# A graph network's edge loop: one stage of each of ten groups per iteration, and a POOL that waits for its own gathers

## The chip, the cores and the metric

The kernel runs on one core of a Trainium2 chip. The engines named here are TensorE (PE, matrix products; PEld is its weight load), VectorE (DVE), ScalarE (ACT), GpSimd (POOL) and SyncE (SP, which here only issues transfers). Each engine works through its own queue of instructions in order; between engines there are semaphores. SBUF is the memory that engines work in, PSUM the small memory that PE writes to. The metric is the device time of one execution in microseconds, as the median of several runs.

## What is computed

One layer of message passing over 200000 edges and 12500 nodes of 64 features, all in float32. `ssp` is softplus minus log 2. Edges are sorted by `dst`; `src` is random.

```python
nodes = node_state[edges].reshape(num_edges, -1)            # rows of src and dst, 128 wide
gates = ssp(edge_state @ We1 + be1) @ We2 + be2
gates = gates * (1.0 - sigmoid(5.0 * (edges_distance - 3.5)))
h = ssp(nodes @ Wn1 + bn1) @ Wn2 + bn2
messages = h * gates
message_sum = zeros_like(node_state).at[edges[:, 1]].add(messages)
# then per node: out = layernorm(2 * x + (ssp(message_sum @ Ws1 + bs1) @ Ws2 + bs2)), eps 1e-5
```

## The kernel before

The edges are cut into 391 groups of 512, each of four slots of 128 edges (one edge per partition). For a group g the stages are these, with the lines of the kernel.

- **gather** (L204): POOL issues one indirect DMA per slot, which fetches 128 rows of x (256 bytes each) by `src_i` into the tile `xg`. A few slots (70 of all) are instead put together column by column from a transposed copy of x, by short copies on DVE and ACT (L259, `columns`): per iteration 8 columns on DVE and 16 on ACT. So most groups issue four gathers, the others three; 1493 in all.
- **load** (L216, L224): SP fetches the edges' features `eT` (every second group) and, for each half group, 42 rows of a table (x times the second half of Wn1, written to DRAM in the early iterations) into `wns`.
- **onehot** (L277, DVE): a 42 wide one-hot of the edge's dst relative to the half group's first dst, beside the gathered row in `xg`.
- **transposes** (L283, PE) of the four slots into the PSUM tile `tx`, and **xcopy** (L291, ACT) of it to SBUF.
- **layer 1** (PE): bias L296, edge part L301, node part L308, into the PSUM tile `z` of 768 columns. Ahead of the node part stands a matmul whose result is not used (L334, `busy_before_node`), or, in early iterations, the product for one chunk of the table.
- **exps** and **logs** (L322, L325, ACT): u = ln(1 + exp(z)); **softplus** (L330, DVE) takes u from SBUF and z from PSUM.
- **layer 2** (PE): bias L347, edge part L354, node part L359, into the PSUM tile `gh`; another unused matmul (L334 with `gh`) ahead of it.
- **hcut** and **message** (L368, L372, DVE): the gate times the cutoff times h, from `gh`.
- **scatter** (L376, PE): the one-hot times the messages, into columns of a later group's `z` that are free; **window** (L396, DVE) adds these 84 columns to `sums` in SBUF, reading them in PSUM.

When all edges of 512 nodes are in `sums`, a node block (L398 to L479) makes their output rows; its eleven parts are spread over iterations by the lists in `BLOCK_STEPS`.

The order is written out by hand. Iteration i of the loop (L688 to L746) holds transposes, layer 1, exps, logs and softplus of group i+1; layer 2, hcut and message of group i; scatter and window of group i−2; gather of group i+3 and load of group i+5. The last groups and the last node block are written out after the loop (L750 to L789). POOL's gathers have no wait of their own in the code except, for the first groups, on transposes; later the eight buffers of `xg` make them wait. PSUM tiles come in pairs: two of `z`, two of `tx`, two of `gh`.

Of the kernel before, what the change touches and what calls it, by code (L numbers as in the profile page):

```python
# [11 lines left out]
I32 = mybir.dt.int32  # L12
# [61 lines left out]
def slots_by_columns(NG):  # L74

    slots, taken = [], set()
    for queue in (1, 0):
        columns, n = COLUMNS[queue], 0
        for g in range(NG - 2):
            if (g - 3 - COLUMNS_FROM + 1) * columns >= (n + 1) * P and not {g - 1, g, g + 1} & taken:  # L80
# [12 lines left out]
def chunk_of(i, NCH):  # L93

    c = i + CHUNKS
    return c if i >= 0 and c < NCH else None


def nodes_ready(g, NCH):

    return min(NCH, CHUNKS * (1 + max(0, (g - LOADS) // CHUNKS))) * P


@with_exitstack
def gnn_resnorm_kernel(ctx: ExitStack, tc: tile.TileContext, a: dict, out: bass.AP, E: int):
# [10 lines left out]
    REST = LOADS + 2  # L116
# [9 lines left out]
    loads = inner.enter_context(tc.tile_pool(name="loads", bufs=LOADS + 2, side="right"))  # L126
# [44 lines left out]
    columns_at = const.tile([P, sum(columns_of)], I32, name="columns_at")  # L171
    wn1_twice = const.tile([P, 2 * D], F32, name="wn1_twice")
# [22 lines left out]
    def gather(g, part=range(K), needs=()):  # L195

        if part[0] == 0:
            xgs[g] = loads.tile([P, K, P], F32, name="xg", bufs=AHEAD + BEHIND)
        xg = xgs[g]
        for k in part:  # L200
# [3 lines left out]
            behind(note(("gather", g), nc.gpsimd.indirect_dma_start(  # L204
                out=xg[:, k, :D], out_offset=None, in_=x,
                in_offset=bass.IndirectOffsetOnAxis(ap=src_i[:, g, k : k + 1], axis=0))), *needs)
            needs = ()
# [3 lines left out]
    def load(g):  # L211
        old = ("scatter", g - LOADS - 4)
# [18 lines left out]
    column_at, columns_done, whole = [[], []], [0, 0], []  # L231
# [32 lines left out]
    def choose(pool):  # L264

        while whole:
            queue, g, k = slot = whole.pop(0)
# [6 lines left out]
    xTs, zs, us, ss, ghs, hs, msgs, scs = ({} for _ in range(8))  # L274
# [14 lines left out]
    def xcopy(g):  # L289
        xT = work.tile([DW, K, P], F32, name="xT", bufs=3)  # L290
        note(("xcopy", g), nc.scalar.copy(xT, xTs[g]))  # L291
        xTs[g] = xT.rearrange("f (t h) e -> f h t e", h=2)

    def layer1_bias(g, *needs):
        zs[g] = z_tile()
# [21 lines left out]
    every, edge, node = slice(0, 3 * HE), slice(0, HE), slice(HE, 3 * HE)  # L317

    def exps(g, part=every):
        if part.start == 0:  # L320
            us[g] = work.tile([P, 3 * HE], F32, name="u")
        nc.scalar.activation(us[g][:, part], z_of(g)[:, part], AF.Exp)  # L322

    def logs(g, part=every):
        nc.scalar.activation(us[g][:, part], us[g][:, part], AF.Ln, bias=one)  # L325

    def softplus(g, part=every):
        if part.start == 0:
            ss[g] = work.tile([P, 3, 2, P], F32, name="s", bufs=3)
        nc.vector.scalar_tensor_tensor(ss[g].rearrange("p i t e -> p (i t e)")[:, part], us[g][:, part], BIG,  # L330
                                       z_of(g)[:, part], OP.min, OP.max)
# [7 lines left out]
    opened = {}  # L339

    def busy_before_layer2(g):
        opened[g + 1] = gh_tile()
        busy(opened[g + 1][:, :P])

    def layer2_bias(g):
        gh = opened.pop(g) if g in opened else gh_tile()
# [19 lines left out]
    def hcut(g):  # L366
        hs[g] = work.tile([P, K, D], F32, name="h")
        nc.vector.tensor_mul(hs[g], ghs[g][:, 1], cut[:, g, :].to_broadcast([P, K, D]))  # L368

    def message(g):  # L370
        msgs[g] = work.tile([P, K, D], F32, name="msg", bufs=3)
# [26 lines left out]
    def node_block(first, n, pool):  # L398
# [7 lines left out]
        def tile3(name):  # L406
            return pool.tile([P, 2, 2, D], F32, name=name, bufs=3)[:p, :nq]
# [4 lines left out]
        def hidden(z):  # L412
            t["z"] = z[:, :HE]
            for q in range(nq):
                nc.tensor.matmul(t["z"], ws1[:, q].rearrange("f o d -> f (o d)"),  # L415
                                 sums[:, first + q * HE : first + (q + 1) * HE], start=q == 0, stop=q == nq - 1,
                                 skip_group_check=True)

        def fetch():
            t["y"] = tile3("y")  # L420
            nc.sync.dma_start(t["y"], x[rows, :].rearrange("(q p k) d -> p q k d", q=nq, k=2))
# [5 lines left out]

        def clamp():
            t["l"], t["zb"] = (pool.tile([P, HE], F32, name=name, bufs=2) for name in ("l_s", "zb"))
            nc.vector.tensor_scalar(t["l"], t["z"], packed["bs1"], BIG, OP.add, OP.min)  # L430
            nc.vector.tensor_scalar(t["zb"], t["z"], packed["bs1"], None, OP.add)
# [8 lines left out]
        def layer2(z):  # L440
            slots = t["l"].rearrange("f (p k) -> f k p", k=2)
            t["u"] = z[:p, :HE].rearrange("p (q k d) -> p q k d", q=2, k=2)
            nc.tensor.matmul(z[:p, :HE], ones3[:, :p], rs3.rearrange("q k d -> q (k d)"), start=True,
                             stop=False, skip_group_check=True)
            for k in range(2):
                nc.tensor.matmul(t["u"][:, :, k, :], slots[:, k, :p], ws2, start=False, stop=k == 1,  # L446
                                 skip_group_check=True)

        def add():
            nc.vector.scalar_tensor_tensor(t["y"], t["y"], 2.0, t["u"][:, :nq], OP.mult, OP.add)  # L450

        def square():
            t["y2"] = tile3("y2")
# [23 lines left out]
        return [Part(None, fetch), Part(hidden, clamp), Part(None, logs), Part(None, center), Part(None, ssp),  # L477
                Part(layer2, add), Part(None, square), Part(None, variance), Part(None, root), Part(None, scale),
                Part(None, store)]  # L479

    def node_part(part):
        if part.tensor:
            part.tensor(gh_tile())
        part.others()

    with tc.manual_schedule():
# [4 lines left out]
        xT = sums[: D + 1, : NCH * P].rearrange("d (c p) -> d c p", p=P)  # L491
# [3 lines left out]
        def load_x(first, last):  # L495
            nc.sync.dma_start(xT[:, first:last, :], a["xT"][:, first:last, :])

        dst_h = prep.tile([P, NR, HE], I32, name="dst_h")
# [5 lines left out]
        nc.sync.dma_start(src_i[:, :HEAD, :], cols[:, :HEAD, :])  # L504
        nc.scalar.dma_start(dst_h, a["dst_h"])
        load_x(0, CHUNKS)
        nc.scalar.dma_start(consts[:, :FIRST], a["consts"][:, :FIRST])
        nc.sync.dma_start(dst_i[:, :HEAD, :], targets[:, :HEAD, :])
# [5 lines left out]
        load_x(CHUNKS, 2 * CHUNKS)  # L514

        for g in range(AHEAD):
            gather(g)
# [24 lines left out]
        for c in range(CHUNKS):  # L542
            nc.tensor.matmul(ps[:, c, :], xT[:, c, :], wnb, start=True, stop=True)
# [4 lines left out]
        spread = prep.tile([P, NR, P], F32, name="spread")  # L548
        base_b = prep.tile([P, NR * P], F32, name="base_b")
# [66 lines left out]

        def highest():
# [10 lines left out]
        def far():  # L628
            ps = tx_tile()
# [13 lines left out]
        def chunk(c, z):  # L643
            if c % CHUNKS == 0:
                tbs[c // CHUNKS] = piece()
            nc.tensor.matmul(z, xT[:, c, :], wnb, start=True, stop=True, skip_group_check=True)
# [6 lines left out]
        cuts = [2 * CHUNKS, 4 * CHUNKS, 6 * CHUNKS, 9 * CHUNKS, 12 * CHUNKS, NCH]  # L653
        beside = {0: [lambda: nc.sync.dma_start(src_i[:, HEAD:, :], cols[:, HEAD:, :])],
                  1: [lambda: nc.sync.dma_start(columns_i, a["columns"]), load_wn1, lambda: load_xh(0)],
                  2: [lambda: load_xh(1), far], 3: [lambda: load_xh(2)], 4: [lambda: load_xh(3), places],
                  5: [lambda: load_x(cuts[0], cuts[1])],
                  6: [lambda: nc.sync.dma_start(dst_i[:, HEAD:, :], targets[:, HEAD:, :])],
                  7: [lambda: load_x(cuts[1], cuts[2])], 10: [lambda: load_x(cuts[2], cuts[3])],
                  13: [lambda: load_x(cuts[3], cuts[4])], 16: [lambda: load_x(cuts[4], cuts[5])]}  # L660
# [6 lines left out]
        with tc.tile_pool(name="finish", bufs=1) as finish:  # L667
            blocks = list(zip(node_blocks(N), block_steps(N, NG)))
            last = NG - 1
            parts, begun, complete, rest = {}, None, 0, []  # L670
# [5 lines left out]
            def behind_by(i):  # L676
                close = last - CLOSE
                return [g for g in ([i - 2] if i <= close else []) + ([i - 1] if i >= close else []) if g >= 0]

            for g in range(LOADS - 1):  # L680
                load(g)
            for g in range(2):
                onehot(g)
            lowest(1, NR)
            everywhere(1, NR)
            clear(0, CHUNKS)
            highest()
# [264 lines left out]
```

## Time and profile before

| | |
|---|---|
| median of 3 runs | 2370.89 us (2367.87 to 3131.28) |
| profiled execution, its own time | 2389.88 us |
| its span | 2388.1 us |
| mean granted clock of PE in it | 0.981 |
| PE busy | 1970.5 us, 83% of the span |
| ACT busy | 1511.2 us, 63% |
| POOL busy | 1417.0 us, 59% |
| DVE busy | 1293.9 us, 54% |
| DMA | 148.63 MB, 62 GB/s |

Times of single rows come from the profiled execution, and are to be set against its own time of 2389.88 us, not against the median. Busy time counts an engine's own operations: a wait, and the issue of a transfer by SP, are not in it. The time that POOL spends on an indirect DMA is the time to issue it; the transfer itself runs on the DMA engines, afterwards or beside. In rows of groups the columns are: line, engine, operation, output and inputs, shapes, number of instructions, busy time and mean in nanoseconds, and then the engine's idle time right ahead of these instructions, with what ended most of it.

### The profile page before, as it was taken

How to read it: one execution, taken by the hardware profiler on the slowest of the kernel's cores; microseconds unless marked ns; L12 is line 12 of the kernel's file. 1: busy time of each engine (PE TensorE's matmuls, PEld its weight loads, DVE VectorE, ACT ScalarE, POOL GpSimd, SP SyncE). 2: the span in 40 equal slices, each digit the busy share in tenths (PEclk: the TensorE clock that was granted, in tenths of full speed). 3: DMA queues.
4: the chain of work that ended last, by engine and by line, in shares of the span. 5: the costliest groups of instructions: out<-in, count | busy, mean ns of one | idle time of the engine just before them, and what ended most of it. 6: DMA issues, size and time to landing. Idle time of an engine off the chain costs nothing.

```text
span 2388.1 us, 48209 instructions
## 1 busy us (share of the span) xinstructions
PE 1970.5 (83%) x12897; PEld 1656.7 (69%) x12897; DVE 1293.9 (54%) x5966; ACT 1511.2 (63%) x7412; POOL 1417.0 (59%) x1497
## 2 busy tenths in 40 slices
PE   6788888888888888888888888888888888888877
PEld 4666677767776776677677667766777767777765
DVE  4355555555555555555555555555555555555544
ACT  3466666666666666666666666666666666666653
POOL 5665665666666666666666666665665666666650
PEclk9799999999999999999999999999999999999988
DMA  6332232322222222222222222222222222222220
GB/s 185 85 91 68 56 75 56 77 61 71 54 57 56 53 59 54 57 56 62 53 59 55 57 58 55 59 59 54 58 58 56 59 57 60 63 57 58 59 50 14
DMA packets 159679, 148.63 MB, mean 62 GB/s; under 512 B 40564, under 2 KB 108949, under 8 KB 159274
## 3 DMA queue, kind: packets, MB, share of 16 engines
q1 hardware_dynamic: 111194, 94.97, 14.4%
q0 software_dynamic: 47776, 49.02, 10.8%
q8 instruction: 109, 1.79, 0.3%
q14 instruction: 166, 1.36, 0.2%
q10 hardware_dynamic: 434, 1.50, 0.2%
HBM read 135.70 MB, written 9.62 MB: 61 GB/s over the span
## 4 chain that ended last, share of the span: by engine, by line
PE 80%; issue 13%; ACT 3%; DVE 2%; another core or an unknown queue 1%; DMA 0%; DVEq 0%; ACTq 0%
PE z L308 18%; PE gh L359 13%; PE z L376 10%; PE tx L283 10%; PE gh L354 7%; PE z L301 6%; PE gh L334 4%; PE gh L347 3%; PE z L296 3%; PE z L334 2%; ACT xT L291 2%; PE tx L415 1%; PE tx L446 1%; PE z L311 1%
## 5 line engine op out<-in xcount | busy, mean ns | idle before, releaser
L204 POOL DMA_INDIRECT xg<-in_x,src_i x1493 | 1416.8, 949 | 919.3 <-PE tx L283 488.8
L308 PE MATMUL z<-xT,wns 106*128 106x256 f32 x1564 | 459.7, 412 | 359.9 <-issue 285.9
L291 ACT COPY xT<-tx 106x512 f32<-106x512 f32 x391 | 229.1, 586 | 779.3 <-PE tx L283 751.1
L259 ACT COPY column<-xh 128x4 uint8 x6016 | 608.7, 193 | 0.0
L308 PEld LDWEIGHTS z<-xT,wns 106*128 106x128 f32 x1564 | 267.8, 193 | 452.4 <-issue 337.7
L368 DVE TENSOR_TENSOR h<-gh,cut 128x256 f32<-128x256 f32 x391 | 165.9, 424 | 747.9 <-PE tx L283 632.2
L359 PE MATMUL gh<-consts,s 128*128 128x64 f32 x3128 | 396.0, 270 | 0.0
L359 PEld LDWEIGHTS gh<-consts,s 128*128 128x128 f32 x3128 | 385.0, 194 | 0.1
L325 ACT ACTIVATE u<-u,one 128x768 f32<-128x768 f32 x392 | 365.8, 933 | 13.4 <-ACT u L322 0.5
L330 DVE SCALAR_TENSOR_TENSOR s<-u,z 128x768 f32<-128x768 f32 x392 | 368.7, 941 | 0.4 <-issue 0.4
L322 ACT ACTIVATE u<-z 128x768 f32<-128x768 f32 x392 | 314.7, 803 | 43.4 <-PE z L308 19.0
L396 DVE TENSOR_TENSOR sums<-sums,z 64x42 f32 x778 | 152.4, 196 | 291.3 <-issue 207.4
L376 PEld LDWEIGHTS z<-xg,msg 128*128 128x128 f32 x1556 | 205.0, 192 | 140.6 <-issue 121.3
L376 PE MATMUL z<-xg,msg 128*128 128x84 f32 x1556 | 265.1, 293 | 15.3 <-DVE msg L372 15.3
L259 DVE COPY column<-xh 128x4 uint8 x2944 | 246.5, 219 | 0.4 <-issue 0.4
L354 PE MATMUL gh<-consts,s 128*128 128x128 f32 x1564 | 243.3, 279 | 1.3 <-DVE s L330 0.8
L283 PE MATMUL tx<-consts,xg 128*106 128x128 f32 x1564 | 238.1, 276 | 0.0
L301 PE MATMUL z<-eT,consts 128*128 128x256 f32 x782 | 237.3, 386 | 0.0
L354 PEld LDWEIGHTS gh<-consts,s 128*128 128x128 f32 x1564 | 210.0, 195 | 2.0 <-DVE s L330 1.1
L283 PEld LDWEIGHTS tx<-consts,xg 128*106 128x106 f32 x1564 | 182.5, 142 | 0.9 <-issue 0.9
L372 DVE TENSOR_TENSOR msg<-gh,h 128x256 f32<-128x256 f32 x391 | 165.8, 424 | 13.4
L334 PEld LDWEIGHTS gh<-consts 128*128 128x128 f32 x778 | 149.5, 195 | 20.5 <-issue 0.3
(109 smaller groups left out, 1456.2 us busy)
## 6 DMA issues: line engine op xcount, KB each, us to landing
eT<-in_eT SPq DMA_DIRECT2D x195, 256.0 KB
xg<-in_x,src_i POOLq DMA_INDIRECT x1493
wns<-table SPq DMA_DIRECT2D x782, 21.0 KB
table<-tb SPq DMA_DIRECT2D x14, 448.0 KB
side<-in_sides SPq DMA_DIRECT2D x70, 64.0 KB
y<-in_x SPq DMA_DIRECT2D x24, 128.0 KB
out<-y SPq DMA_DIRECT2D x24, 128.0 KB
xh<-in_xh SPq DMA_DIRECT2D x2, 781.5 KB
```

The lines of the kernel that those rows point to most:

```text
L204: behind(note(("gather", g), nc.gpsimd.indirect_dma_start(out=xg[:, k, :D], out_offset=None, in_=x, in_offset=bass.IndirectOffsetOnAxis(ap ...
L259: copy(column_tiles[slot].bitcast(U8)[:, 4 * r : 4 * r + 4], xh[:, bass.ds(column_at[queue][j] - xh_at, 4)])
L283: ins = nc.tensor.transpose(tx[:, k, :], xgs[g][:, k, :DW], ident)
L301: nc.tensor.matmul(zs[g][:, 0, :HE], we1.rearrange("a h d -> a (h d)"), eTs[g], start=False, stop=True, skip_group_check=True)
L308: nc.tensor.matmul(zn, wns[:, g % REST, h, :], xTs[g][:, h], start=True, stop=not chosen, skip_group_check=True)
L322: nc.scalar.activation(us[g][:, part], z_of(g)[:, part], AF.Exp)
L325: nc.scalar.activation(us[g][:, part], us[g][:, part], AF.Ln, bias=one)
L330: nc.vector.scalar_tensor_tensor(ss[g].rearrange("p i t e -> p (i t e)")[:, part], us[g][:, part], BIG, z_of(g)[:, part], OP.min, OP.max)
L334: nc.tensor.matmul(z, we1.rearrange("a h d -> a (h d)"), ident, start=True, stop=True, skip_group_check=True)
L354: nc.tensor.matmul(v[:, 0, t], ss[g][:, 0, t, :], we2, start=False, stop=False, skip_group_check=True)
L359: nc.tensor.matmul(ghs[g][:, 1, 2 * t + h, :], ss[g][:, 1 + h, t, :], wn2, start=False, stop=h == 1 and t == 1, skip_group_check=True)
L376: ins = nc.tensor.matmul(sc, msgs[g][:, 2 * t : 2 * t + 2, :].rearrange("p h f -> p (h f)"), xgs[g][:, 2 * t : 2 * t + 2, D:DW], start=t = ...
```

## The change

Every iteration of the loop now holds one stage of each of ten groups, each a fixed number of iterations behind the transposes (`LAGS`). What one engine makes in an iteration, the next engine takes in a later one. The loop runs on until the last node block is done; the code written out after it, `BLOCK_STEPS` and `CLOSE` are gone.

- PSUM tiles are read by one engine each. `tx` and `z` are read by ACT alone: a new `keep` copies z (768 columns), the 84 columns of sums and, where there is one, a chunk's or node block's 128 columns to the SBUF tile `c`. Softplus and window, on DVE, read `c`. `gh` is read by DVE alone.
- The first gather of a group waits for the last gather of the group before to have landed (`PACE = "landing"`), and for the transposes of five groups before (`GATE`). `xg` has 12 buffers.
- Loads are issued three groups ahead (`FETCH`), behind the same transposes.
- The unused matmul ahead of layer 2 is gone.
- `COLUMNS`: 16 columns per iteration on DVE and 8 on ACT, instead of 8 and 16; the number of slots stays 70.
- Node blocks are cut finer: `take` copies the block's sums on DVE, then hidden layer in two halves, layer 2 once per 256 nodes, each product in the spare columns of `z`.
- Before the loop: the first load of `src_i` holds 8 rows instead of 64, the gathers of the first groups are part of the loop (which begins at i = −3), and some work on the groups' bases moves into iterations 1 to 4.

```diff
-LOADS = 5
+FIRST_ROWS = 8
+FREE = 3
+REST = 7
-PREPARE = 5
-BEHIND = 5
-CLOSE = 12
-BLOCK_STEPS = ((2, 3, 4, 4, 6, 7, 8, 9, 10, 14), (2, 3, 3, 4, 5, 6, 7, 8, 9, 10), (1, 2, 1, 2, 3))
-COLUMNS = (8, 16)
+LAGS = dict(xcopy=1, z=2, exps=3, softplus=4, layer2=5, message=6, sums=7, window=9)
+BUFS = AHEAD + LAGS["sums"] + 2
+GATE = AHEAD + 2
+FETCH = 3
+PACE = "landing"
+PAUSE = 1
+COLUMNS = (16, 8)
...
-    def gather(g, part=range(K), needs=()):
...
+    def gather(g):
+
+        xgs[g] = loads.tile([P, K, P], F32, name="xg", bufs=BUFS)
+        xg, needs, n = xgs[g], [("transposes", g - GATE)], 0
+        if PACE == "landing":
+            needs.append(("last", g - 1))
+        for k in range(K):
             if padding(g, k) or (g, k) in by_columns:
                 nc.vector.memset(xg[:, k, :D], 0.0)
                 continue
+            ins = note(("gather", g), nc.gpsimd.indirect_dma_start(
                 out=xg[:, k, :D], out_offset=None, in_=x,
+                in_offset=bass.IndirectOffsetOnAxis(ap=src_i[:, g, k : k + 1], axis=0)))
+            behind(ins, *needs)
+            needs, n = [], n + 1
+        made["last", g] = [ins]
...
     def load(g):
-        old = ("scatter", g - LOADS - 4)
+        old = ("transposes", g - GATE)
...
+    def keep(z, n, summed, extra):
+
+        ends = (0, 3 * HE, 3 * HE + 2 * W, 3 * HE + 2 * W + P)
+        held = [n is not None, summed is not None, bool(extra)]
+        c, at = None, 0
+        while at < 3:
+            end = at
+            while end < 3 and held[end]:
+                end += 1
+            if end > at:
+                c = work.tile([P, ends[3]], F32, name="c") if c is None else c
+                nc.scalar.copy(c[:, ends[at] : ends[end]], z.rearrange("p b e -> p (b e)")[:, ends[at] : ends[end]])
+            at = end + 1
...
+    def softplus(g):
+        ss[g] = work.tile([P, 3, 2, P], F32, name="s")
+        nc.vector.scalar_tensor_tensor(ss[g].rearrange("p i t e -> p (i t e)"), us[g], BIG, cs[g], OP.min, OP.max)
...
-            for i in range(-1, last - 1):
...
+            i = -AHEAD
+            while i <= NG + lag["window"] or blocks:
+                zt = z_tile()
+                n = i - lag["z"]
...
+                at(load, i + FETCH)
+                at(gather, i + AHEAD)
+                at(layer1_bias, n, ("load", n))
+                summed = i - lag["sums"]
+                at(scatter, summed, zt[:, 1, HE : HE + 2 * W])
+                at(layer2_bias, i - lag["layer2"])
+                at(layer2, i - lag["layer2"])
+                at(layer1_edge, n)
...
+                if free and 0 <= n < NG:
+                    busy_before_node(n)
+                at(layer1_node, n)
+                at(transposes, i, ("gather", i), ("onehot", i))
+
+                at(xcopy, i - lag["xcopy"])
+                at(exps, i - lag["exps"])
+                extra = keep(*kept)
+                at(logs, i - lag["exps"])
...
+                at(softplus, i - lag["softplus"])
+                at(hcut, i - lag["message"])
+                at(message, i - lag["message"])
+                at(onehot, i + 1)
+                at(window, i - lag["window"])
```

More of the change, by code (lines that the diff above doesn't have):

```diff
@@ L667, in gnn_resnorm_kernel @@
         with tc.tile_pool(name="finish", bufs=1) as finish:
-            blocks = list(zip(node_blocks(N), block_steps(N, NG)))
-            last = NG - 1
-            parts, begun, complete, rest = {}, None, 0, []
+            blocks = [[first, n, step, None, 0] for (first, n), step in zip(node_blocks(N), block_steps(N, NG))]
+            kept, chunked, kept_part, waiting = (None, None, None, None), None, None, None
+            lag = LAGS
             def at(f, g, *more):
@@ L730, in gnn_resnorm_kernel @@
[L730 to L733 removed]
+                for queue in (1, 0):
+                    if 0 <= i < NG:
+                        read_columns(i, queue)
+                        columns(i, queue, finish)
+                if 0 <= i < NG:
+                    choose(finish)
                 for action in beside.get(i, []):
                     action()
[L736 to L739 removed]
@@ L740, in gnn_resnorm_kernel @@
-                if blocks and complete >= blocks[0][1]:
-                    steps = next(steps for steps in BLOCK_STEPS if i + steps[-1] < last - 1)
-                    for n, part in zip(steps, begun):
-                        parts.setdefault(i + n, []).append(part)
-                    rest = begun[len(steps) :]
-                    blocks.pop(0)
-                    begun = None
-            assert len(blocks) == 1 and begun and not parts
-            begun.pop(2).others()
-            transposes(last, ("load", last), ("gather", last), ("onehot", last))
@@ L865, in gnn_resnorm_kernel @@
         for block in node_blocks(N):
[L866 removed]
+            for _, part in node_block(*block, o):
                 node_part(part)
```

315 lines of the change are left out of this document (131 added, 184 removed).

## The prediction

> **What bounds the kernel now.** The first view is the page: busy times, costliest groups, and the chain that ended last.
>
> ```profile
> PE 1970.5 (83%) x12897; PEld 1656.7 (69%) x12897; DVE 1293.9 (54%) x5966; ACT 1511.2 (63%) x7412; POOL 1417.0 (59%) x1497
> ...
> PE 80%; issue 13%; ACT 3%; DVE 2%; another core or an unknown queue 1%; DMA 0%; DVEq 0%; ACTq 0%
> ...
> L204 POOL DMA_INDIRECT xg<-in_x,src_i x1493 | 1416.8, 949 | 919.3 <-PE tx L283 488.8
> ...
> L291 ACT COPY xT<-tx 106x512 f32<-106x512 f32 x391 | 229.1, 586 | 779.3 <-PE tx L283 751.1
> ...
> L368 DVE TENSOR_TENSOR h<-gh,cut 128x256 f32<-128x256 f32 x391 | 165.9, 424 | 747.9 <-PE tx L283 632.2
> ```
>
> At first sight TensorE is the bound: busiest, 80% of the chain, and named by every long wait. But ACT, DVE and POOL all stand for some 750 to 919 us "for PE", and PE itself is idle for 17%. So I looked at one ordinary stretch, POOL first, where each row is a start, a duration and the idle time ahead of it.
>
> ```profile
> 730.08 0.94 POOL L204 DMA_INDIRECT xg<-in_x,src_i  x1 [0.30 <-issue]
> 732.45 0.95 POOL L204 DMA_INDIRECT xg<-in_x,src_i  x1 [1.43 <-PE tx L283]
> 733.70 0.94 POOL L204 DMA_INDIRECT xg<-in_x,src_i  x1 [0.30 <-issue]
> 734.95 0.94 POOL L204 DMA_INDIRECT xg<-in_x,src_i  x1 [0.30 <-issue]
> 736.20 0.94 POOL L204 DMA_INDIRECT xg<-in_x,src_i  x1 [0.30 <-issue]
> 738.54 0.94 POOL L204 DMA_INDIRECT xg<-in_x,src_i  x1 [1.40 <-PE tx L283]
> 739.79 0.95 POOL L204 DMA_INDIRECT xg<-in_x,src_i  x1 [0.31 <-issue]
> 741.04 0.94 POOL L204 DMA_INDIRECT xg<-in_x,src_i  x1 [0.30 <-issue]
> 743.29 0.95 POOL L204 DMA_INDIRECT xg<-in_x,src_i  x1 [1.30 <-PE tx L283]
> ```
>
> A gather comes every 1.25 us, and after a group's last one POOL pauses 1.3 to 1.43. Four gathers make 738.54 − 732.45 = 6.09 us, three make 4.75. Next, what the other engines do in one such pause.
>
> ```profile
> 731.17 0.38 PE L334 MATMUL z<-consts 128*128 128x128 f32 x2
> 732.14 0.42 DVE L368 TENSOR_TENSOR h<-gh,cut 128x256 f32<-128x256 f32 x1 [2.74 <-PE tx L283]
> ...
> 732.27 0.59 ACT L291 COPY xT<-tx 106x512 f32<-106x512 f32 x1 [2.34 <-PE tx L283]
> ```
>
> ```profile
> core 0: us, PE busy (x) PEld busy (x) DVE busy (x) ACT busy (x) POOL busy (x), PEclk, DMA share, GB/s
> ...
> 731.02:731.70 0.68, 0.54 (x4) 0.32 (x2) 0.00 (x0) 0.00 (x0) 0.00 (x1) 1.00 0.00 0
> 731.70:731.90 0.20, 0.00 (x0) 0.00 (x0) 0.00 (x0) 0.00 (x0) 0.00 (x0) 1.00 0.66 133
> 731.90:732.15 0.25, 0.00 (x0) 0.00 (x0) 0.01 (x1) 0.00 (x0) 0.00 (x0) 1.00 0.09 25
> 732.15:732.45 0.30, 0.00 (x0) 0.00 (x0) 0.30 (x1) 0.18 (x1) 0.00 (x0) 1.00 0.00 0
> ```
>
> Between 731.70 and 731.90 nothing computes; only the last gather's packets run. They are over by 732.15, 1.13 us after POOL's end at 731.02, and just then DVE, ACT and (at 732.45) POOL restart together, though the program lets DVE and ACT wait here for PE alone, which had finished long before. So I read the iteration as paced already by POOL's issues and the landing of the group's last gather, and the "PE" waits as that landing under another name. Then work taken from PE or ACT buys nothing; only POOL's pause does. Whether the compute engines could bind instead, I read from a steady stretch:
>
> ```profile
> 1000.00:2000.00 1000.00, 842.11 (x5592) 709.33 (x5592) 556.75 (x2619) 657.37 (x3275) 611.74 (x645) 0.99 0.25 58
> ...
> 1000.00:2000.00 1000.00, 159.32 (x169) 0.99 0.25 58
> ```
>
> The second row is L330 alone: 169 iterations, 5.92 us each, with PE busy 4.98, ACT 3.89, DVE 3.29 in each.
>
> **The change part by part.** The base is the profiled execution, 2389.9 us (span 2388.1), 19 us above the median of 2370.9 that is forecast; I subtract these 19 at the end.
>
> *PE.* The busy matmul ahead of layer 2 goes:
>
> ```profile
> L334 PE MATMUL gh<-consts 128*128 128x128 f32 x778 | 152.7, 277 | 0.0
> L322 ACT ACTIVATE u<-z 128x768 f32<-128x768 f32 x392 | 314.7, 803 | 43.4 <-PE z L308 19.0
> L330 DVE SCALAR_TENSOR_TENSOR s<-u,z 128x768 f32<-128x768 f32 x392 | 368.7, 941 | 0.4 <-issue 0.4
> L259 ACT COPY column<-xh 128x4 uint8 x6016 | 608.7, 193 | 0.0
> L259 DVE COPY column<-xh 128x4 uint8 x2944 | 246.5, 219 | 0.4 <-issue 0.4
> ```
>
> 152.7/391 = 0.39 less, 4.59 per iteration. *ACT* gains the copy of z (852 columns; priced by L322's 803 ns for 768: 0.89) and gives up 8 columns (8 × 0.193 = 1.54): 3.24. *DVE* gains 8 columns (8 × 0.219 = 1.75): 5.04, its other operations keeping their widths. All lie below the 6.09 of a four-gather iteration, and each stage has an iteration to itself, so I cost them at nothing; POOL's issue hides them. If that cover went, the dearest is DVE. The three-gather iteration at 4.75 is below DVE's 5.04, but the buffers (12 of xg) spread this over the mean of 5.92. SP's queue issues as many loads as before, at i+3 instead of i+5; behind a load that now waits for transposes of two iterations back stand later loads and the node blocks' fetches and stores. Layer 1 reads a load five iterations after its issue, some 30 us, so this too is at nothing; without that lead PE would wait for the table's rows. Per node block DVE copies 512 columns of sums (under L330's 0.94, 25 blocks: 24 us, inside DVE's slack). What is late next, when the PE-named stalls go, is POOL itself.
>
> *POOL.* The gathers number 1493 in both, so 391 groups and 1102 pauses inside groups. Of the 919.3 idle, 1102 × 0.30 = 331 lie inside groups and 6.2 ahead of the first:
>
> ```profile
> 6.66 1.08 POOL L204 DMA_INDIRECT xg<-in_x,src_i  x1 [6.20 <-DMA src_i<-in_src_l]
> ...
> L204 POOL DMA_INDIRECT xg<-in_x,src_i x1493: 938/945/1163, 6.7 to 2335.6; - x187
> ```
>
> The other 582 over 390 boundaries are 1.49 each. After the change a group's first gather waits in plain words for the group before to have landed. Behind it on POOL's queue stand only more gathers, three iterations ahead of their use; transposes wait for them only if POOL falls back by as much. Its second wait, for transposes two iterations back, is met long before. The new pause isn't in the trace. It cannot be less than about the landing, 1.13. Lower end: POOL restarts 0.30 after the packets' end, as it does after the others' restart: 1.43. Upper end: the landing of all the gather's parts is told later than the packets end. No row shows that lag; I price it like the step POOL needs between two instructions, 0.30, with 0.07 to spare: 1.80. I take 1.70, near the upper end, because 1.43 is where the restart is released before this wait exists, and a wait for every part can only add to it. 390 × (1.70 − 1.49) = **+82**.
>
> The Trainium skill (DMA: Bandwidth & Descriptors, "Anatomy of one DMA — SWDGE (gpsimd) path") puts the semaphore update at about 100 ns behind the write receipt. By that the pause would be an estimated 1.43 + 0.10 = 1.53 and the sum would end near 2396; no row here splits the landing so.
>
> *Ends.* The first src_i load is cut from 64 to 8 rows per lane: −2 (between −4 and 0; it still waits for a DMA). The prologue is crowded:
>
> ```profile
> 0.00:50.00 50.00, 26.83 (x111) 20.22 (x112) 22.41 (x70) 14.13 (x17) 23.96 (x29) 0.90 0.68 195
> 65.00:75.00 10.00, 8.38 (x30) 6.56 (x30) 0.00 (x0) 1.53 (x2) 7.44 (x8) 0.50 0.14 28
> 2336.50:2388.10 51.60, 37.80 (x228) 30.66 (x227) 26.69 (x78) 18.48 (x33) 0.01 (x1) 0.83 0.05 13
> ```
>
> At a DMA share of 0.68 instead of 0.25 a landing takes longer; 29 gathers are some 8 groups, and about 1.25 more for each is +10 (0 to +30). Tail: 51.6 us follow the last gather. Afterwards three full iterations at PE's 4.59 and nine that lose a stage each (half, 2.3) are 34.5, and some nine small steps of the last node block under L330's 0.94 add 8.5: 43, so −9 (35 to 52).
>
> *Contention.* Softplus and the window's adds now read both inputs from SBUF beside POOL. The row of xg above has the gathers' durations as smallest, median and longest, and one DVE operation of this kind runs beside gathers already:
>
> ```profile
> 1204.94 0.95 POOL L204 DMA_INDIRECT xg<-in_x,src_i  x1 [0.30 <-issue]
> ...
> 1205.04 0.33 DVE L277 TENSOR_TENSOR xg<-consts,rel 128x168 f32<-128x168 f32 x1
> ```
>
> That gather took 0.95 with the DVE operation starting inside it. I charge 7 ns (945 − 938) per gather: +10; at most 1163 − 938 = 0.22 for one gather per group, +86. The Trainium skill (SBUF — State Buffer, "Who interferes with whom") says that a DVE instruction with two SBUF inputs contends with a GpSimd instruction that reads SBUF, which speaks against this change. By that a gather could be held for a whole softplus (rival D); the row of 1204.94 doesn't agree.
>
> Sum: 2389.9 + 82 − 2 + 10 − 9 + 10 = 2481 profiled, less 19: **2462**, forecast 2460. With a pause of 1.80 it is 2501, and with half of the 76 by which contention could still grow 2539; with 1.43, +10 in place of both additions' 20, it is 2346.
>
> **The rivals.**
> *Restart no later than today (B).* The landing is told as soon as the packets end, pause 1.43 to 1.49: 2346 to 2380. For it: everything restarts within 0.3 us of the packets' end already. Against: this is a release of other engines, not a wait for all of one gather. That the change doesn't do what it says (the transposes bind, landing never last) falls here too: POOL's pace as it is.
> *Faster (E).* Nothing is released late, so every boundary gets the 1.30 seen ahead of 743.29, and the few long closing pauses vanish: 390 × (1.30 − 1.49) = −74, −2, −15 in the tail: 2299 profiled, 2280. It decides from a pause under 1.39: 390 × 0.10 = 39, with the ends' 11 about 2% in all. Against: 1.30 stands after a three-gather group, and the explicit wait can't undercut the landing.
> *Much slower (C).* PE gets more idle time per iteration (6.36 − 4.59 against 5.92 − 4.98) and may lose its clock: row 65:75 shows 0.50 granted. At half clock PE needs 9.1 against 6.4: +2.7 per iteration. A hundred iterations of that are +270, about 2730. It decides from a clock below 4.59/6.4 = 0.72. Against: 0.99 over 1000 us with idle stretches in every iteration.
> *POOL held by DVE (D).* One gather of each group waits out a whole softplus, 0.94: 391 × 0.94 = +368 in place of the 10 charged, 2820. For it: softplus is nearly three times as long as the L277 operation of 1204.94. Against: that gather shows no delay, and the longest gather of all is 1163.
>
> **How the numbers follow.** Forecast 0.54, B 0.21, E 0.15, C 0.06, D 0.04. Forecast and B hold 0.75; half of E (pauses down to 1.37, 2310) brings it past 0.8. So 2310 to 2540. A measurement here tells about 2% (47 us, 2323 to 2418) from no change. Faster: E, 0.15. Same: B and the forecast's low edge (pauses under 1.59), 0.21 + 0.07 = 0.28. Slower: the rest, 0.57.
>
> **What would show it.** In the profile afterwards: POOL's pauses at group ends of some 1.7, released by a DMA; its other pauses still 0.30; L204 still 1493 with a mean near 949; the four-gather iteration near 6.36; PE's share falling to some 75%, ACT's and DVE's waits no longer carrying the time. Wrong if the pause stays at or under 1.45 (B, E), if POOL's gathers lengthen past 1 us (D), if the granted clock falls (C), or if DVE ends up without idle time.

## The result, and the profile after

The changed kernel took 2829.0 us in the median (2813.4 to 2833.0) against 2369.4 before: a ratio of 1.193, 95% interval 1.187 to 1.199. The forecast was 2460, in a range of 2310 to 2540. The direction was right; the size was not, by a factor of five. Ratios, and the time in the last row of the table below, leave out executions that ran slower than the others of the same kernel: one of the kernel before (3131 us) and two of that row (2494 and 2496).

The page of the changed kernel, the lines that answer to those quoted before:

```profile
span 2826.3 us, 47346 instructions
...
PE 2484.3 (88%) x12157; PEld 1958.6 (69%) x12157; DVE 1564.2 (55%) x9136; ACT 1478.0 (52%) x4740; POOL 1474.8 (52%) x1497
...
PE 39%; POOL 11%; DMA 11%; issue 10%; DVE 9%; ACT 2%; DVEq 1%; POOLq 0%
...
L209 POOL DMA_INDIRECT xg<-in_x,src_i x1493 | 1474.6, 988 | 1309.1 <-issue 371.7
L304 ACT COPY xT<-tx 106x512 f32<-106x512 f32 x391 | 229.2, 586 | 1301.7 <-PE tx L296 1132.8
```

The whole difference of the spans, 2826.3 − 2388.1 = +438 us, stands in POOL's row and in what follows its last instruction. POOL's idle time went from 919.3 to 1309.1 (+390), its busy time from 1416.8 to 1474.6 (+58), and the tail after the last gather, which the view of the tile `xg` places, got shorter (2826.3 − 2783.3 − 0.95 = 42.0 against 51.6, −10):

```profile
L209 POOL DMA_INDIRECT xg<-in_x,src_i x1493: 942/947/2136, 6.8 to 2783.3; - x187
```

390 + 58 − 10 = 438. Such a sum closes for any engine that works to the end, so it places the loss and does not yet say that POOL sets the pace. The 1102 pauses inside groups are still 0.30 each, so (1309.1 − 331 − 6.8) / 390 = 2.49 us stand between two groups, where it was 1.49. In POOL's timeline of the changed kernel (start, duration, idle time ahead):

```profile
1498.85 1.58 POOL L209 DMA_INDIRECT xg<-in_x,src_i  x1 [0.30 <-issue]
1502.74 1.02 POOL L209 DMA_INDIRECT xg<-in_x,src_i  x1 [2.30 <-PE tx L296]
1504.07 0.95 POOL L209 DMA_INDIRECT xg<-in_x,src_i  x1 [0.30 <-issue]
1505.32 0.95 POOL L209 DMA_INDIRECT xg<-in_x,src_i  x1 [0.31 <-issue]
1508.54 0.95 POOL L209 DMA_INDIRECT xg<-in_x,src_i  x1 [2.28 <-DVE s L359]
1509.79 0.94 POOL L209 DMA_INDIRECT xg<-in_x,src_i  x1 [0.30 <-issue]
1511.04 0.95 POOL L209 DMA_INDIRECT xg<-in_x,src_i  x1 [0.30 <-issue]
1512.29 0.95 POOL L209 DMA_INDIRECT xg<-in_x,src_i  x1 [0.31 <-issue]
1515.94 0.95 POOL L209 DMA_INDIRECT xg<-in_x,src_i  x1 [2.70 <-PE tx L296]
...
1523.39 0.95 POOL L209 DMA_INDIRECT xg<-in_x,src_i  x1 [2.29 <-DMA xg<-in_x,src_i]
```

The pause is 2.28 to 2.30 again and again, whatever name stands behind it (DVE's softplus, PE's transposes, the gather's DMA): a sign that none of the changing names is the cause, but the one thing that is the same each time, the landing of POOL's own last gather. Some pauses are longer (2.70), which brings the mean to 2.49. These go with other transfers: from 50 us on, 0.05 MB move during a pause under 2.4 us in the mean, 0.21 MB and more during one over 2.5. PE in the same place, from the timeline of all engines:

```profile
1502.06 0.40 PEld L296 LDWEIGHTS tx<-consts,xg 128*106 128x106 f32 x4 [2.47 <-issue]
1502.09 0.62 PE L296 MATMUL tx<-consts,xg 128*106 128x128 f32 x4 [2.10 <-DVE scaled L500]
```

POOL's gather had ended at 1498.85 + 1.58 = 1500.43. PE stood for the same landing: by then 800 gathers had been issued, the last of them the last of group 208 (groups count from 0), and 832 transposes made, four for each of the 208 groups before that one. So POOL's lead of three iterations was used up, and here POOL does set the pace; at 86 boundaries (every fourth) the lead is never more than one group. PE begins the transposes 1.63 later; POOL begins 2.30 later, another 0.68. The packets were over sooner (columns as for the stretches in the prediction; the last two figures are the DMA share and GB/s):

```profile
1501.13:1501.33 0.20, 0.00 (x0) 0.00 (x0) 0.12 (x1) 0.00 (x0) 0.00 (x0) 1.00 0.92 143
1501.33:1501.53 0.20, 0.00 (x0) 0.00 (x0) 0.19 (x2) 0.00 (x0) 0.00 (x0) 1.00 0.08 21
1501.53:1501.73 0.20, 0.00 (x0) 0.00 (x0) 0.17 (x2) 0.00 (x0) 0.00 (x0) 1.00 0.01 0
```

That is about 1.1 after POOL's end, as in the kernel before.

The steady stretch, all of it and softplus (L359) alone:

```profile
1000.00:2000.00 1000.00, 889.49 (x4416) 702.36 (x4414) 561.15 (x3349) 535.87 (x1758) 531.54 (x542) 0.79 0.20 48
...
1000.00:2000.00 1000.00, 136.48 (x143) 0.79 0.20 48
```

143 iterations in 1000 us, 6.99 each instead of 5.92; and PE's granted clock is 0.79 instead of 0.99. So two suspects for the loss stand side by side: POOL's longer pause, and a PE that lost its clock. The new order of stages is a third.

### The profile page after: what moved, and what is told of

Its sections match the earlier page's. It is cut to its first block, busy times and chain, and to the rows that moved or that the text cites. A ratio compares the mean times of both kernels' runs of the same rounds, so it can differ in the third digit from the quotient of the medians.

```text
span 2826.3 us, 47346 instructions
## 1 busy us (share of the span) xinstructions
PE 2484.3 (88%) x12157; PEld 1958.6 (69%) x12157; DVE 1564.2 (55%) x9136; ACT 1478.0 (52%) x4740; POOL 1474.8 (52%) x1497
## 4 chain that ended last, share of the span: by engine, by line
PE 39%; POOL 11%; DMA 11%; issue 10%; DVE 9%; ACT 2%; DVEq 1%; POOLq 0%
POOL xg L209 11%; DMA xg<-in_x,src_i 11%; PE gh L381 8%; PE z L320 6%; PE tx L296 5%; PE gh L376 5%; PE z L398 5%; PE z L313 3%; DVE s L359 3%; PE gh L369 2%; DVE column L269 2%; PE z L308 1%; DVE h L390 1%; PE z L474 1%; PE z L362 1%
## 5 line engine op out<-in xcount | busy, mean ns | idle before, releaser
L209 POOL DMA_INDIRECT xg<-in_x,src_i x1493 | 1474.6, 988 | 1309.1 <-issue 371.7
L359 DVE SCALAR_TENSOR_TENSOR s<-u,c 128x768 f32<-128x768 f32 x391 | 373.7, 956 | 850.0 <-PE gh L381 448.3
L269 DVE COPY column<-xh 128x4 uint8 x6016 | 488.7, 191 | 282.2 <-issue 280.6
L381 PE MATMUL gh<-consts,s 128*128 128x64 f32 x3128 | 518.3, 324 | 0.0
L381 PEld LDWEIGHTS gh<-consts,s 128*128 128x128 f32 x3128 | 512.9, 248 | 0.0
L347 ACT COPY c<-z 128x852 f32<-128x852 f32 (+4 forms) x402 | 353.5, 879 | 12.9 <-PE z L474 5.9
L376 PE MATMUL gh<-consts,s 128*128 128x128 f32 x1564 | 349.1, 358 | 0.0
L376 PEld LDWEIGHTS gh<-consts,s 128*128 128x128 f32 x1564 | 259.6, 236 | 115.4 <-issue 114.8
L313 PE MATMUL z<-eT,consts 128*128 128x256 f32 x782 | 338.3, 523 | 0.0
L269 ACT COPY column<-xh 128x4 uint8 x2944 | 317.1, 207 | 10.9 <-issue 8.6
L418 DVE TENSOR_TENSOR sums<-sums,c 64x42 f32 x782 | 153.6, 196 | 50.8 <-issue 45.0
L369 PE MATMUL gh<-row,ones 3*128 3x512 bf16 x391 | 177.8, 455 | 0.0
```

The costliest lines, as they stand in the source:

```text
L209: ins = note(("gather", g), nc.gpsimd.indirect_dma_start(out=xg[:, k, :D], out_offset=None, in_=x, in_offset=bass.IndirectOffsetOnAxis(ap= ...
L269: copy(column_tiles[slot].bitcast(U8)[:, 4 * r : 4 * r + 4], xh[:, bass.ds(column_at[queue][j] - xh_at, 4)])
L313: nc.tensor.matmul(zs[g][:, 0, :HE], we1.rearrange("a h d -> a (h d)"), eTs[g], start=False, stop=True, skip_group_check=True)
L347: nc.scalar.copy(c[:, ends[at] : ends[end]], z.rearrange("p b e -> p (b e)")[:, ends[at] : ends[end]])
L376: nc.tensor.matmul(v[:, 0, t], ss[g][:, 0, t, :], we2, start=False, stop=False, skip_group_check=True)
L381: nc.tensor.matmul(ghs[g][:, 1, 2 * t + h, :], ss[g][:, 1 + h, t, :], wn2, start=False, stop=h == 1 and t == 1, skip_group_check=True)
```

## The experiments

Theory W is that the wait itself costs the time. Its rivals are P (the lost clock of PE sets the pace, and POOL follows) and S (the new order of stages). A fourth question came up with the first runs: on some chips the kernel before takes 1994 us, on others 2365. The table gives beside each time that of the kernel before on the same chip; where the text compares other times, it says on which kind of chip they were taken.

| kernel | time, us | kernel before beside it | mean pause of POOL between groups, us | clock |
|---|---|---|---|---|
| before + wait for its own landing | 2767.6 | 1994.4 | 2.53 | 0.876 |
| the same, other run | 2765.9 | 1998.3 | 2.53 | 0.885 |
| changed, no landing wait | 2044.6 | 1994.4 | 0.32 | 0.973 |
| the same, other run | 2401.2 | 2367.2 | 1.36 | 0.870 |
| changed, wait two groups back | 2050.5 | 1994.4 | 0.32 | 0.967 |
| changed, wait for the last gather but one | 2407.4 | 1994.4 | 1.38 | 0.877 |
| changed + 4 unused matmuls | 2808.6 | 2364.6 | 2.48 | 0.924 |
| changed, again | 2827.8 | 2364.6 | 2.48 | 0.781 |
| changed, again | 2832.2 | 1998.3 | 2.49 | 0.785 |
| before, again | 2366.0 | 2364.6 | 1.45 | 0.976 |
| before, again | 1995.5 | 1998.3 | 0.48 | 0.994 |
| changed, no wait, softplus from PSUM | 2445.5 | 2367.2 | 1.62 | 0.850 |

The mean pause is POOL's idle time in the row of its gathers, less 331 for the pauses inside groups and less the first wait (6 to 7 us), over 390.

**The wait alone, in the kernel before.**

```diff
     def gather(g, part=range(K), needs=()):
...
+        needs, ins = list(needs) + [("last", g - 1)], None
         for k in part:
...
+        made["last", g] = [ins]
```

> The kernel before, with one thing added: a group's first gather waits for the last gather of the group before to have landed. Theory W (the wait itself costs the time: POOL's pause between groups goes from 1.49 to the 2.3 or more seen in the changed kernel): 390 x 0.8 = +312 us or more, some 2680 to 2760, pauses near 2.3, whatever the rest of the program looks like. Rival P (PE's lost clock, 0.78 in place of 0.98, sets the pace of the changed kernel and POOL only follows): this kernel keeps PE's busy matmuls and its clock, so the wait costs little, 2370 to 2450. Rival S (the new order of stages is what costs): 2370 to 2450 as well, with the clock unchanged.

It took 2767.6 us, on a chip where the kernel before takes 1994.4: a ratio of 1.388 (1.385 to 1.390). The row of its gathers:

```profile
L205 POOL DMA_INDIRECT xg<-in_x,src_i x1493 | 1415.1, 948 | 1322.5 <-issue 365.1
```

All the busy matmuls and the old order of stages are there, and the pause is 2.53; the time lies just above what W had given. Once more:

> The kernel before with the landing wait alone, once more. It took 2768 us on a chip where the kernel before takes 1994. If the chip is one where the kernel before takes 2365, theory W still gives 2760 to 2800, since the pause of the wait (2.3 and more) takes the place of the pause of 1.43 and is not added to it; were both paid, it would be 2768 + 375 = 3140.

2765.9 against 1998.3, the same; the chip was again one on which the kernel before is quick, so the added wait has not been seen in the kernel before on a chip where that takes 2365. P and S fall here as main causes: with neither the new stages nor a clock under 0.87 the kernel comes within some 60 us of the changed one (2829.0), and the gathers' own length makes up as much (988 against 948 ns, 1474.6 − 1415.1 = 59.5).

**The changed kernel without the wait.** One word: `PACE = "none"`.

> The changed kernel without the wait for its own landing; the wait for the transposes of five groups before stays. Theory W: the pause falls back to 1.5 or less, 2829 - 390 x 0.8 to 1.0 = 2440 to 2520, or less still if POOL never pauses. Rival P: the clock stays near 0.78, PE needs 6.35 us per iteration, so no less than 391 x 6.35 + some 60 = 2540, and more likely 2700 to 2829. Rival S: about 2829.

2044.6 against 1994.4, 1.028 (1.023 to 1.034), with PE busy for 95% of the span:

```profile
PE 1945.3 (95%) x12157; PEld 1565.4 (77%) x12157; DVE 1542.4 (76%) x9136; ACT 1478.2 (73%) x4740; POOL 1532.8 (75%) x1497
...
L209 POOL DMA_INDIRECT xg<-in_x,src_i x1493 | 1532.6, 1027 | 462.6 <-issue 335.3
```

This is below the figures of all three; W had allowed for it in the case that POOL never pauses, and POOL hardly does (0.32, the step between any two issues). On a chip of the other kind:

> The changed kernel without the wait for its own landing, once more, in the hope of a chip on which the kernel before takes 2365 and pauses 1.4 us between groups. Theory W: POOL's gate (transposes of two iterations back) is loose enough that the pause falls to that of the kernel before or less: 2050 to 2450. If on such a chip the other engines' signals stop POOL whatever the program, the pause comes out near 1.4 and the time near 2400; if the loose gate frees POOL, 0.30 and 2050. If the chip is one where the kernel before takes 1994: 2045 again.

2401.2 against 2367.2, 1.016 (1.012 to 1.019). Here POOL pauses 1.36, though its program no longer waits for the landing. Nor is the gate always what it waits for: at 46 of 86 boundaries (every fourth), the transposes of five groups before had been over for 3 us or more when the group's first gather began. Against the changed kernel on chips of this kind (2829.0) the wait is worth 2829.0 − 2401.2 = 428 us of the 460 lost; all the rest of the change costs 34, under the 2% from which a change counts as one.

**The wait two groups back.**

```diff
-            needs.append(("last", g - 1))
+            needs.append(("last", g - 2))
```

> The changed kernel, its wait put one group further back: a group's first gather waits for the last gather of two groups before, which has landed long ago. If a wait on a landed gather costs by its mere presence (a fixed step of POOL after such a wait), pauses near 0.3 + 0.5 to 0.7, or as in the kernel without the wait but 0.5 more. If only the landing itself costs: the same time as without the wait, within 1%.

2050.5, and POOL's row says 462.6 idle, to the digit that of the kernel without the wait. A wait on a landing that has happened is free.

**The wait one gather earlier.**

```diff
-        made["last", g] = [ins]
+        made["last", g] = [all_of[-2]]
```

> The changed kernel, its wait put one gather earlier: a group's first gather waits for the last but one gather of the group before. That one lands one gather's step (1.25 us) sooner. Theory W with pause = landing + a fixed restart: the pause is shorter by 1.25, some 2.3 - 1.25 = 1.05, unless another wait takes over; time 2829 - 390 x 1.0 to 1.4 = 2280 to 2440. Rivals P and S: about 2829, as PE or the order sets the pace.

2407.4, in the upper part of W's range. In POOL's timeline of this kernel:

```profile
1508.22 0.94 POOL L209 DMA_INDIRECT xg<-in_x,src_i  x1 [1.17 <-PE gh L382]
1509.47 0.94 POOL L209 DMA_INDIRECT xg<-in_x,src_i  x1 [0.30 <-issue]
1510.71 0.94 POOL L209 DMA_INDIRECT xg<-in_x,src_i  x1 [0.30 <-issue]
1511.96 0.94 POOL L209 DMA_INDIRECT xg<-in_x,src_i  x1 [0.30 <-issue]
1514.04 0.94 POOL L209 DMA_INDIRECT xg<-in_x,src_i  x1 [1.13 <-DVE chosen L285]
...
1518.98 0.94 POOL L209 DMA_INDIRECT xg<-in_x,src_i  x1 [1.08 <-DVE y L480]
```

Pauses of 1.08 to 1.17: shorter than 2.28 by 1.11 to 1.20, nearly one gather's step of 1.25. So the ordinary pause follows the landing that it waits for, plus a rest that stays nearly the same. The mean is 1.38, because longer pauses are mixed in.

**More work for PE.** In `layer2_bias`, ahead of the bias:

```diff
         gh = gh_tile()
+        for _ in range(4):
+            busy(gh[:, :P])
```

> The changed kernel with four unused matmuls more ahead of layer 2 in every iteration (the kernel before had one there), so that PE idles less: 4 x 0.39 = 1.6 us more work per iteration at full clock, in an iteration of 7.2 us of which PE needs 4.6 at full clock. Theory W: the time stays within 2% of the changed kernel's, with the clock up from 0.78. Rival P (PE at its low clock sets the pace): if the clock rises to 0.95 or more the time falls by at least 10%; if it stays at 0.78, the time grows by 391 x 1.6 / 0.78 = 800 us.

2808.6 against 2364.6, 1.189 (1.183 to 1.195); beside the changed kernel's 2827.8 of the same chip that is 0.7% less. The clock came back for the most part (0.902 to 0.924 in the four runs, short of the 0.95 that the expectation named), and the time did not:

```profile
core 0: 2801.3 us, clock 0.924
```

```profile
L209 POOL DMA_INDIRECT xg<-in_x,src_i x1493 | 1442.1, 966 | 1306.3 <-issue 361.7
```

P falls: 1306.3 us of idle POOL at 0.924, 1309.1 at 0.778. With more work for PE in the same pace the clock rises, so the lower clock comes of PE standing for POOL and does not set the pace. The small gain fits POOL's shorter gathers (1442.1 against 1474.6 busy, −32).

**The kernels themselves, on other chips.**

> The kernel before once more, with its profile: beside the first four experiments it took 1994 us, and not the 2370 us of its first profile. If its pause of 1.43 between groups is a property of the chip that ran it, not of the program, then a run of 1994 shows the same busy times and POOL pauses of 0.30 at the group ends (390 x 1.13 = 440 us less than the 582 us of before, of which other engines take some back), and a run of 2370 shows 1.43 again. If instead other things got faster, the pauses stay and busy times fall.

> The kernel before, for its profile. On a chip where it takes 1994: POOL's pauses at group ends 0.30 like those inside groups, idle time of POOL near 919 - 390 x 1.13 = 480 us, busy times as before. On a chip where it takes 2365: the first profile again.

The first gave 2366.0, with pauses of 1.45; the second 1995.5. That one's page and POOL's timeline:

```profile
PE 1943.8 (97%) x12897; PEld 1634.5 (82%) x12897; DVE 1314.6 (66%) x5966; ACT 1508.1 (76%) x7412; POOL 1419.0 (71%) x1497
...
PE 92%; ACT 4%; DMA 1%; DVE 1%; issue 1%; ACTq 0%; DVEq 0%
...
L204 POOL DMA_INDIRECT xg<-in_x,src_i x1493 | 1418.8, 950 | 523.8 <-issue 348.7
```

```profile
727.52 0.94 POOL L204 DMA_INDIRECT xg<-in_x,src_i  x1 [0.30 <-issue]
728.76 0.95 POOL L204 DMA_INDIRECT xg<-in_x,src_i  x1 [0.30 <-PE z L376]
730.01 0.94 POOL L204 DMA_INDIRECT xg<-in_x,src_i  x1 [0.30 <-issue]
```

The same program, with busy times that agree within 2%, and hardly a pause between the groups: 523.8 us of idle POOL instead of 919.3. With the pause gone, PE is the bound, busy for 97%. So the pause of 1.43 in the first profile is not in the program. It goes with the chip, or with something that held for all runs on it.

> The changed kernel once more, beside the kernel before on one chip. Its pause is its own landing and the restart after it, 2.3 us, which no other engine's signal sets. Theory W: 2780 to 2830 on any chip, whether the kernel before takes 1994 or 2370 beside it. If the chip sets it instead: some 375 us less on a chip where the kernel before takes 1994, 2450.

> The changed kernel, beside the kernel before of the same chip. Theory W: 2780 to 2830, pauses of 2.2 to 2.4, on either kind of chip. If the chip decided, 2450 where the kernel before takes 1994.

2827.8 where the kernel before takes 2364.6, and 2832.2, in one run, where it takes 1998.3; the mean pauses are 2.48 and 2.49. The changed kernel takes the same time on both kinds of chip, as W has it, and the pause of 1.43 is not paid on top of its own; what the change costs depends on the chip, a ratio of 1.19 or of 1.42 (2832.2 / 1998.3).

**Softplus from PSUM, without the wait.**

```diff
-LAGS = dict(xcopy=1, z=2, exps=3, softplus=4, layer2=5, message=6, sums=7, window=9)
+LAGS = dict(xcopy=1, z=2, exps=3, softplus=3, layer2=5, message=6, sums=7, window=9)
...
-        nc.vector.scalar_tensor_tensor(ss[g].rearrange("p i t e -> p (i t e)"), us[g], BIG, cs[g], OP.min, OP.max)
+        nc.vector.scalar_tensor_tensor(ss[g].rearrange("p i t e -> p (i t e)"), us[g], BIG,
+                                       z_of(g), OP.min, OP.max)
```

with layer 2 and the transposes ahead of layer 1 on PE, z no longer copied, and softplus behind the window on DVE.

> As the kernel without the wait, but softplus takes z from PSUM again, one iteration earlier and last but the columns on DVE; z is not copied (the 84 columns of sums still are), and PE does layer 2 and the transposes ahead of layer 1. Theory D (an operation of DVE with two inputs in SBUF holds back a gather that begins beside it): without the wait the gathers took 1027 ns in the mean against 949 in the kernel before; here they are back under 960, 1493 x 0.07 = 100 us less for POOL, and the time falls by up to that, to 1945 to 2045 where the kernel without the wait takes 2045. Rival: the gathers' length has another cause (more columns on DVE, the pace itself) and stays over 1000.

The gathers are short again, and the time is not:

```profile
L209 POOL DMA_INDIRECT xg<-in_x,src_i x1493 | 1416.5, 949 | 970.0 <-issue 349.9
```

2445.5 against 2367.2 beside it, and 2401.2 for the kernel without the wait on the same chip, whose gathers took 988. The shorter gathers bought nothing, and the mean pause rose from 1.36 to 1.62, 390 × 0.26 = +101 us. In both kernels POOL is three to four groups ahead of the transposes on this chip, so its issue is not what the others wait for. The program differs in more than the inputs: z is free only after softplus, and PE's order is another. Which of these stretched the pauses was not told apart, and on a quick chip, where the length of the gathers would count, this kernel was not run.

How a gather is held, in the timeline of the changed kernel without the wait (second run):

```profile
1501.50 0.89 DVE L359 SCALAR_TENSOR_TENSOR s<-u,c 128x768 f32<-128x768 f32 x1
...
1501.78 1.42 POOL L209 DMA_INDIRECT xg<-in_x,src_i  x1 [0.30 <-issue]
```

The gather begins inside a running softplus, which ends at 1502.39; it takes 1.42 instead of 0.94. With z in PSUM, in the last kernel of the table, it is not held:

```profile
1555.25 0.95 DVE L359 SCALAR_TENSOR_TENSOR s<-u,z 128x768 f32<-128x768 f32 x1
...
1555.54 0.94 POOL L209 DMA_INDIRECT xg<-in_x,src_i  x1 [0.30 <-issue]
```

This does not hang on the other edits. Of the gathers that begin with 0.4 us or more of a softplus still to run, 97 in the changed kernel take 1.44 in the median and up to 1.85; with z in PSUM, 174 in this kernel and 132 in the kernel before (the profile of 1995.5) take 0.95 at most. The 169 gathers of the changed kernel that begin inside a softplus account for 54 of its 58 us. So the longer gathers do come from softplus's second input in SBUF.

## Why the prediction was wrong, step by step

**What bounds the kernel** was read rightly for the changed kernel: POOL's lead is used up there, its pause accounts for the loss, and neither PE's clock nor its load moved the time. For the kernel before the reading "paced already by POOL's issues" does not hold. At every one of 86 boundaries (every fourth), POOL began a group four groups ahead of the transposes, on the slower chips and on the quicker ones alike, and at the 40 where the scatters were counted that of eight groups before was the last one made. That is as far as the eight buffers let it go, so no transposes waited for its issue. On the quicker chips PE is the bound; on the slower ones DVE, ACT and POOL do go on only about when the last gather's packets are over, as the prediction saw, but what holds them was not found. The 1.49 that the sum sets against the new pause was thus another wait. That the difference of the two could still be multiplied by 390 follows from POOL's wait for its landing taking the other's place.

**The step that failed** is "I take 1.70", with its upper end of 1.80, and with it the term of +82: measured were a mean of 2.49 and a term of +390. The packets were over about 1.1 after POOL's end, as assumed (1.13); what lies behind them was mis-sized. For the lag of the signal and POOL's restart together the 1.70 leaves 0.57 and the upper end 0.67; they took about 1.2, which makes the ordinary pause of 2.30. In the row shown PE began on the landed gather 1.63 after POOL's end and POOL 0.68 later (medians where PE's start shows in the pause: 1.67 and 0.65; in the kernel before with the wait 1.89 and 0.47, with the same sum), so both parts were too small; since PE's own restart is in the first figure, no row divides them exactly. The rest to 2.49, about 74 us, are longer pauses. Some 9 us of these lie in the first 50 us, for which the prediction had its +10; the others it had not forecast. The mistake was to call 1.80 an upper end when no row of the trace held a wait of POOL for its own gather: it was a guess at both lags with 0.07 to spare. The Trainium skill's 100 ns behind the write receipt (DMA: Bandwidth & Descriptors, "Anatomy of one DMA — SWDGE (gpsimd) path"), from which I had worked out an estimated pause of 1.53, is not contradicted by this: it starts only at the receipt, and the same section lets the receipt take most of a fixed cost of about 2 us, which the estimate left out. No run here shows the receipt by itself; the pause so estimated was too short by 0.8.

**Contention**: +10 in the sum, at most +86; measured +58. The rule that I weighed (Trainium skill, SBUF — State Buffer, "Who interferes with whom") holds here in this form: softplus with two inputs in SBUF delays a gather that begins while it runs (1.42 against 0.94), and with one input in PSUM the gathers are back at 949. The row that I set against the rule, 1204.94, had the DVE operation begin after the gather: it was the wrong order of the two, and told nothing of the other one. The profile before had rows of the right order:

```profile
207.21 0.33 DVE L277 TENSOR_TENSOR xg<-consts,rel 128x168 f32<-128x168 f32 x1
207.25 1.11 POOL L204 DMA_INDIRECT xg<-in_x,src_i  x1 [0.30 <-issue]
```

Rival D had the mechanism right and its price too high (368), since it held one gather of each of 391 groups, and only 169 gathers of the changed kernel begin inside a softplus.

**Ends**: the tail was forecast at −9 and came out at −10. The first gather did not begin sooner (6.8 against 6.7; forecast −2).

**Costed at nothing**: the copies of z, the columns moved to DVE, the cut node blocks and PE's missing matmuls. Right while POOL paces with its wait. Without the wait the rest of the change costs 34 us on a chip like that of the forecast; what makes up these 34 was not separated, as POOL does not pace there. On a quick chip it costs 50 us. There POOL issues without a stop (all but 2 of the 1492 gaps between gathers are about 0.30) and sets the pace, and its longer gathers (1532.6 against 1418.8 busy, +114) more than account for the 50; so this price is contention's.

**The rivals.** B and E needed a pause of 1.49 or less and fell at once. C foresaw that PE would lose its clock by waiting, and it did, to 0.778; but it stayed above the 0.72 from which C was to decide, and the price of 270 us is refuted, since the same pause stands at a clock of 0.924. D's 2820 lies nearest to the measured time, by luck: the lengthening of the gathers that it prices came out at 58 us.

## What to carry to other kernels

A wait of an issuing engine for its own last transfer costs the whole way to the signal and back, here 2.3 us against 0.30 between two issues without it, and where that engine sets the pace, with one group of transfers per iteration, it is paid in every iteration; a wait one group further back was free. Where no row holds the wait that a change adds, the upper end of its price has to be taken from a row of the same kind of wait, or be left wide: a pause that others show at the same place is a different thing. Whether an engine sets the pace is read from its lead over the engine that takes its results: at its limit, as in the kernel before, it does not. And a lower clock beside a longer iteration may be a symptom; a kernel with the clock restored tells, as it did here.

## What the runs showed of the hardware

The kernel before takes 1994 to 1998 us on some chips and 2365 to 2370 on others, with busy times that agree within 2% on every engine. On the slower ones DVE and ACT start in bunches 0.9 to 1.3 us after POOL's last gather of a group, about when its packets are over, and POOL's pause is mostly 1.2 to 1.5 (mean 1.45 to 1.49); on the quicker ones it is mostly 0.30 (mean 0.48). The changed kernel without its wait shows the same split (2044.6 and 2401.2), the one with the wait does not (2827.8, 2832.2). What differs between the chips was not found, and no run here was made for it.

In the changed kernel POOL needed about 0.7 us more than PE to go on after the landing of a gather, in waits that had to be waited out; a wait on a gather long landed cost nothing (462.6 us of idle POOL with it and without).

An indirect DMA that POOL begins while softplus runs on DVE with both inputs in SBUF took up to 1.85 us; begun inside the same operation with one input in PSUM, 0.4 us or more before its end, it took 0.95 at most.
